# Four heads' quarters at once, or two: the order of score products and masks in a latent-attention layer

## The chip, the cores and the metric

The kernel runs on one core of a Trainium2 chip. The metric is the device time of one execution in microseconds. Three runs of the kernel before took 2292.64, 2293.26 and 2297.32 us, with a median of 2293.26 us. A core has a matrix engine (TensorE, "PE" in the profile; its weight loads are "PEld"), a vector engine (VectorE, "DVE"), a scalar engine (ScalarE, "ACT"), a general engine (GpSimd, "POOL") and a queue engine (SyncE, "SP") that here only issues DMAs. Each engine works through its own instructions in order; engines wait for each other through semaphores.

## The reference

Eight stages in a row work on x of shape (2, 1024, 128) in fp32. Each adds its result to x, and each begins with a layer norm of x: attention with one shared key and value head (layer "a"), a dense FFN with fp6-quantized operands, causal attention ("b"), the same dense FFN, causal attention whose keys and values come from a 32-wide latent ("c"), a mixture of 8 experts, causal attention with biases ("d"), and the mixture of experts again. All attentions have 16 heads of width 64 and 1024 positions. The layer that matters here is "c":

```python
latent_bll = jnp.einsum('bld,dc->blc', x_bld, Wkv_down)
k_blhd = jnp.einsum('blc,chk->blhk', latent_bll, Wk_up)
v_blhd = jnp.einsum('blc,chk->blhk', latent_bll, Wv_up)
attn = jnp.einsum('bqhd,bkhd->bhqk', q_blhd, k_blhd) / jnp.sqrt(jnp.asarray(HD, dtype=x_bld.dtype))
mask = (jnp.arange(l)[None, :] <= jnp.arange(l)[:, None])[None, None]
attn = jax.nn.softmax(jnp.where(mask, attn, neg_inf), axis=-1)
```

The scores of a head have the width 64 as their sum, but k is a product with the 32-wide latent, so the kernel folds Wk_up into the query projection once. A score is then a sum over 32 numbers, and one score product fills only a quarter of TensorE's 128 rows.

## The kernel before

**Units and steps.** An attention layer is worked in 16 units: two batches times eight pairs of heads. The units of layer c are c0 to c15 here; the profile's names (sc_c, pr_c, nmax_c) carry only the letter. A causal unit has five steps, each with one or two tiles of 128 queries, so that a step has about the same number of keys: the query tiles [7], [6, 0], [5, 1], [4, 2] and [3] (CAUSAL_STEPS). Layer c thus has 80 steps.

**One step.** The function `scores` issues, for the two heads h of the pair, the score products into two tiles `sc`, one of 128 x 1024 fp32 in PSUM for each head. There are two such buffers in all (pool ps_s), so head h of a step has to wait until ScalarE has read head h of the step before. Each head's products come in two halves, `lower` and `upper`, which write different PSUM banks. In layers a, b and d a half uses 64 of the 128 rows (ROWS), so two products run side by side; in layer c it uses a quarter (QUARTERS[2 * h + half], 32 rows), so that head 0 has quarters 0 and 1 and head 1 has quarters 2 and 3. `in_turn` deals out the products of several generators in turn, one of each. In fp32 each product appears in the profile as two matmuls (two passes).

The causal mask is added on TensorE: a product of an identity with a matrix of -2^100 above the diagonal is accumulated onto the scores of the diagonal tile. In layers b and d it uses a half of the rows and is part of the generators. In layer c (`mask`, L653) it uses all 128 rows in bf16, one matmul for each query tile of the step.

Behind each head's products, VectorE takes the negated maximum of each row (`nmax`, L682), ScalarE takes the exponential with that as bias and sums it (L697), VectorE inverts the sum (`rec`, L704, one for both heads, issued in the next step), and GpSimd scales the exponentials (L708). Two steps later the scaled tiles are transposed: blocks of 32 on VectorE into `slots` (L778), moved to their places by 16 DMAs on SyncE's queue (`blocks_moved`, L753), and the remaining tiles on TensorE (`pp`, L794), copied out by ScalarE. The product with the values (`av`, L845 in layer c) follows.

**What sets the order.** The order in each engine's queue is written out by hand in the loop over steps: transposes of the step two back with `normalize` of the last step inside them, the additions to x, `scores` and `exponentials` of the new step, the output products, a part of the next unit's projection, parts of the "side" work (norms, FFN or experts of the other batch), and up to four value products (`weigh_some(4)`). VectorE therefore runs transposes, rec and then the maxima of the new step, and TensorE runs pp, the scores, the output product or projection, side work, av.

**The lines of the change.** In `scores`, layer c (`latent`) issues the products of both heads, all four generators in turn, then the masks of head 0 and of head 1, before the loop over heads. In that loop the other layers issue their two generators for the head, and every layer issues the maxima.

Of the kernel before, what the change touches and what calls it, by code (L numbers as in the profile page):

```python
# [36 lines left out]
def kernel(ctx: ExitStack, tc: tile.TileContext, a: dict, out: bass.AP):  # L37
# [571 lines left out]
    def keys(u, qt):  # L609
        return qt + 1 if layers[u[0]]["causal"] else NT  # L610
# [12 lines left out]
    def scores(st):  # L623


        u, qts, at, k = st["u"], st["qts"], st["at"], st["k"]
        causal, latent = layers[u[0]]["causal"], layers[u[0]]["kind"] == "latent"
        sc = [ps_s.tile([P, 2 * QB], F32, tag="sc", name=f"sc_{k}_{h}") for h in range(2)]

        def operands(h, half):  # L630
            if latent:
                return QUARTERS[2 * h + half], qT[u][0], kT[u]
            x = 1 if h != half else 0
            return ROWS[half], qT[u][x], kT[u][x]

        def product(h, half, qt, k0, k1, diagonal):
            r, q, kk = operands(h, half)
            yield nc.tensor.matmul(  # L638
                sc[h][:, at[qt] + k0 : at[qt] + k1], lhsT=q[r, qt * P : (qt + 1) * P],
                rhs=kk[r, k0:k1], start=True, stop=not diagonal,  # L640
            )
            d = at[qt] + qt * P
            for f in range(P // DH if diagonal and not latent else 0):
                yield nc.tensor.matmul(  # L644
                    sc[h][:, d + f * DH : d + P], lhsT=unit[r, f, :], rhs=over[r, f, f * DH :],
                    start=False, stop=(f == P // DH - 1),
                )

        def mask(h):

            for qt in reversed(qts):
                d = at[qt] + qt * P
                nc.tensor.matmul(  # L653
                    sc[h][:, d : d + P], lhsT=ident_b, rhs=over_all, start=False, stop=True
                )

        def lower(h):

            yield from product(h, 0, qts[0], 0, QB - at[qts[0]], False)
            if len(qts) == 2:  # L660
                yield from product(h, 0, qts[1], 0, keys(u, qts[1]) * P, True)

        def upper(h):
            mid = QB - at[qts[0]]
            yield from product(h, 1, qts[0], mid, keys(u, qts[0]) * P, causal)

        def in_turn(gens):
            while gens:
                gens = [g for g in gens if next(g, None) is not None]

        if latent:
            in_turn([half(h) for h in range(2) for half in (lower, upper)])
            for h in range(2):
                mask(h)
        nmaxs = []
        for h in range(2):
            if not latent:
                in_turn([lower(h), upper(h)])
            nmax = small.tile([P, len(qts)], F32, tag="nmax", name=f"nmax_{k}_{h}")
            for n, qt in enumerate(qts):  # L680
                c = slice(at[qt], at[qt] + keys(u, qt) * P)
                nc.vector.tensor_reduce(  # L682
                    out=nmax[:, n : n + 1], in_=sc[h][:, c], axis=AX.X, op=ALU.max, negate=True
                )
            nmaxs.append(nmax)
        return sc, nmaxs
# [356 lines left out]
    lower = const.tile([P, NE, NE], F32, tag="lower", name="lower")  # L1043
# [46 lines left out]
    for step, (n, u, qts, i, total) in enumerate([*steps, *[(None, None, None, 0, 1)] * 4]):  # L1090
# [48 lines left out]
        if new:  # L1139
            sc, nmaxs = scores(new)  # L1140
            for h in range(2):
                exponentials(new, h, sc[h], nmaxs[h])
            last_step.append(new)
            waiting.append(new)
# [89 lines left out]
```

## Time and profile before

| | |
|---|---|
| median of three runs | 2293.26 us |
| profiled execution, its own time | 2291.09 us |
| its span, first to last instruction | 2289.4 us |
| mean clock granted to TensorE | 0.971 |
| layer c, from c0's first score product to the last step's end | 1178.4 to about 1656 us |
| units of layer c, first product to first product | 25.5 us (c6) to 36.4 us (c13) |

The profiled execution is 2.2 us below the median. Times inside the profile are counted from the first instruction. The page splits the span in 40 slices, about 57 us each; layer c is the slices 21 to 29. A row of the timeline merges neighbouring instructions of the same kind; its first column is the start, its second the length, and in square brackets stands how long the engine had been idle before and what ended that. In the waits, the three numbers are microseconds in all, times, and the longest. TensorE's clock falls to half for stretches of 3.4 or 6.8 us, most of them in layer c; a matmul then takes twice as long.

### The profile page before, as it was taken

What the parts mean: (1) busy time and instruction counts of PE and PEld (TensorE: products, weight loads), DVE (VectorE), ACT (ScalarE), POOL (GpSimd) and SP (SyncE); (2) the same over time, 40 slices, a digit from 0 to 9 for tenths busy, and PEclk for the clock granted to TensorE, in tenths of its full rate; (3) what the DMA queues carried; (4) which work ended last, traced back from release to release, by engine and by line L of the source; (5) the groups of instructions that cost most, each with busy time, mean ns of one, the idle gap of its engine ahead of it and who ended that gap; (6) DMA issues with size and microseconds to landing.
All of it is one profiled execution on the core that took longest, in us unless ns stands there. A gap on an engine that the chain in (4) does not pass through costs nothing.

```text
span 2289.4 us, 43111 instructions
## 1 busy us (share of the span) xinstructions
PE 2103.5 (92%) x14833; PEld 1231.8 (54%) x14833; DVE 1691.4 (74%) x2375; ACT 1492.9 (65%) x3340; POOL 1294.1 (57%) x1723
## 2 busy tenths in 40 slices
PE   6999999999998999999997888888889999999986
PEld 2454444444445666666654444444455666656663
DVE  7978999999886876678668877766766656766544
ACT  5777777667865666666655566655666557666652
POOL 4757777668765555465546655555644446544441
PEclk9999999999999999999998899999999999999998
DMA  5666666556676666666655556644665556646450
GB/s 140 145 150 155 159 154 149 131 131 150 153 189 152 149 160 162 161 155 154 147 131 124 129 130 139 141 109 103 171 157 133 122 119 158 161 118 145 111 139 10
DMA packets 144632, 320.42 MB, mean 140 GB/s; under 512 B 48288, under 2 KB 58784, under 8 KB 144416
## 3 DMA queue, kind: packets, MB, share of 16 engines
q1 hardware_dynamic: 144416, 317.67, 58.8%
q8 instruction: 120, 1.97, 0.4%
q14 instruction: 96, 0.79, 0.1%
HBM read 10.27 MB, written 2.10 MB: 5 GB/s over the span
## 4 chain that ended last, share of the span: by engine, by line
PE 58%; DVE 12%; SPq 9%; POOL 6%; ACT 5%; DMA 5%; issue 5%; DVEq 0%; ACTq 0%; POOLq 0%
SPq L753 9%; PE sc_a L638 7%; PE av_a L850 7%; PE av_d L850 5%; PE sc_b L638 5%; PE av_b L850 4%; PE sc_d L638 4%; DVE slots L778 4%; DMA prT<-slots 4%; ACT pr_c L697 2%; PE sc_c L638 2%; POOL pr_a L708 2%; DVE nmax_d L682 2%; DVE nmax_c L682 2%; PE pp_d L794 2%
## 5 line engine op out<-in xcount | busy, mean ns | idle before, releaser
L708 POOL TENSOR_SCALAR pr_a<-pr_a,rec_a 128x1024 f32<-128x1024 f32 x256 | 284.1, 1122 | 189.3 <-DVE rec_a L704 183.4
L697 ACT ACTIVATE pr_a<-sc_a,nmax_a 128x1024 f32<-128x1024 f32 x256 | 283.2, 1111 | 162.5 <-DVE nmax_a L682 94.1
L708 POOL TENSOR_SCALAR pr_d<-pr_d,rec_d 128x1024 f32<-128x1024 f32 (+7 forms) x256 | 187.0, 748 | 265.9 <-DVE rec_d L704 265.9
L682 DVE TENSOR_REDUCE nmax_a<-sc_a 128x1 f32<-128x1024 f32 x256 | 300.0, 1212 | 49.7 <-PE sc_a L638 49.6
L708 POOL TENSOR_SCALAR pr_b<-pr_b,rec_b 128x1024 f32<-128x1024 f32 (+7 forms) x256 | 190.0, 760 | 216.0 <-DVE rec_b L704 215.8
L682 DVE TENSOR_REDUCE nmax_d<-sc_d 128x1 f32<-128x1024 f32 (+7 forms) x256 | 177.4, 750 | 173.0 <-PE sc_d L644 172.3
L708 POOL TENSOR_SCALAR pr_c<-pr_c,rec_c 128x1024 f32<-128x1024 f32 (+7 forms) x256 | 188.4, 754 | 195.7 <-DVE rec_c L704 195.7
L697 ACT ACTIVATE pr_c<-sc_c,nmax_c 128x1024 f32<-128x1024 f32 (+7 forms) x256 | 186.5, 739 | 146.2 <-DVE nmax_c L682 118.1
L697 ACT ACTIVATE pr_b<-sc_b,nmax_b 128x1024 f32<-128x1024 f32 (+7 forms) x256 | 186.6, 739 | 142.8 <-DVE nmax_b L682 102.8
L697 ACT ACTIVATE pr_d<-sc_d,nmax_d 128x1024 f32<-128x1024 f32 (+7 forms) x256 | 186.6, 739 | 131.6 <-DVE nmax_d L682 117.6
L778 DVE STREAM_TRANSPOSE slots<-pr_a 128x1792 f32<-128x1792 f32 x128 | 261.0, 2039 | 12.7 <-POOL pr_a L708 8.7
L638 PE MATMUL sc_a<-k_a,q_a 64*128 64x512 f32 x512 | 261.3, 629 | 1.7 <-ACT pr_a L697 1.7
L682 DVE TENSOR_REDUCE nmax_b<-sc_b 128x1 f32<-128x1024 f32 (+7 forms) x256 | 177.1, 749 | 111.6 <-PE sc_b L644 110.6
L638 PE MATMUL sc_a<-k_a,qx_a 64*128 64x512 f32 x512 | 258.6, 629 | 0.0
L682 DVE TENSOR_REDUCE nmax_c<-sc_c 128x1 f32<-128x1024 f32 (+7 forms) x256 | 177.3, 750 | 97.7 <-PE sc_c L653 97.7
L850 PE MATMUL av_a<-prT,v_a 128*64 128x256 f32 x1792 | 223.2, 388 | 3.7 <-DMA prT<-slots 1.4
L850 PEld LDWEIGHTS av_a<-prT,v_a 128*64 128x64 f32 x1792 | 121.1, 137 | 122.7 <-issue 70.2
L638 PE MATMUL sc_d<-k_d,q_d 64*128 64x512 f32 (+3 forms) x416 | 158.9, 494 | 0.3 <-ACT pr_d L697 0.3
L638 PE MATMUL sc_b<-k_b,q_b 64*128 64x512 f32 (+3 forms) x416 | 158.8, 494 | 0.0
L638 PE MATMUL sc_b<-kx_b,qx_b 64*128 64x512 f32 (+3 forms) x416 | 153.3, 488 | 0.1
L638 PE MATMUL sc_d<-kx_d,qx_d 64*128 64x512 f32 (+3 forms) x416 | 153.2, 488 | 0.2
L778 DVE STREAM_TRANSPOSE slots<-pr_b 128x2048 f32<-128x2048 f32 (+1 forms) x64 | 121.8, 1903 | 12.0 <-DMA prT<-slots 8.8
(408 smaller groups left out, 4765.1 us busy)
## 6 DMA issues: line engine op xcount, KB each, us to landing
prT<-slots SPq DMA_DIRECT2D x768, 128.0 KB, 2.3
prT<-slots SPq DMA_DIRECT2D x832, 112.0 KB, 2.2
prT<-slots SPq DMA_DIRECT2D x768, 96.0 KB, 2.1
qx_b<-q_b SPq DMA_DIRECT2D x32, 256.0 KB, 3.6
kx_b<-k_b SPq DMA_DIRECT2D x32, 256.0 KB, 3.6
qx_d<-q_d SPq DMA_DIRECT2D x32, 256.0 KB, 3.7
kx_d<-k_d SPq DMA_DIRECT2D x32, 256.0 KB, 3.5
x<-in_x SPq DMA_DIRECT2D x4, 256.0 KB, 3.8
```

The costliest lines, as they stand in the source:

```text
L638: yield nc.tensor.matmul(sc[h][:, at[qt] + k0 : at[qt] + k1], lhsT=q[r, qt * P : (qt + 1) * P], rhs=kk[r, k0:k1], start=True, stop=not dia ...
L682: nc.vector.tensor_reduce(out=nmax[:, n : n + 1], in_=sc[h][:, c], axis=AX.X, op=ALU.max, negate=True)
L697: nc.scalar.activation(tiles_of(st, qt)[:, :, h, :], sc[:, c].rearrange("p (k q) -> p k q", q=P), AF.Exp, bias=nmax[:, n : n + 1], accum_o ...
L708: nc.gpsimd.tensor_scalar(out=pt, in0=pt, scalar1=rec[:, h, n : n + 1], scalar2=1.0, op0=ALU.mult, op1=ALU.mult,)
L753: nc.sync.dma_start(out=o, in_=x)
L778: nc.vector.transpose(dst, tiles[:, :n].rearrange("p k h (r q) -> p (k h) r q", q=32),)
L794: nc.tensor.transpose(pt[:, h, kt - k0, :], tiles[:, kt, h, :], ident)
L850: nc.tensor.matmul(shaped(av[ROWS[h], n], t0), lhsT=vs[u][:, kt, h, :], rhs=moving(h, kt, t0), start=(kt == 0), stop=(kt == nkt - 1),)
```

## The change

In layer c, each head now has its own turn: its lower and upper halves side by side (two quarters of TensorE's rows), its masks right behind, and its maxima. Only then do the products of head 1 follow. The number, the shapes and the operands of all instructions stay the same, and nothing outside `scores` is touched; in layers a, b and d nothing changes.

```diff
@@ -668,14 +668,11 @@
             while gens:
                 gens = [g for g in gens if next(g, None) is not None]
 
-        if latent:
-            in_turn([half(h) for h in range(2) for half in (lower, upper)])
-            for h in range(2):
-                mask(h)
         nmaxs = []
         for h in range(2):
-            if not latent:
-                in_turn([lower(h), upper(h)])
+            in_turn([lower(h), upper(h)])
+            if latent:
+                mask(h)
             nmax = small.tile([P, len(qts)], F32, tag="nmax", name=f"nmax_{k}_{h}")
             for n, qt in enumerate(qts):
                 c = slice(at[qt], at[qt] + keys(u, qt) * P)
```

On TensorE's queue the order of a step is before: the passes of both heads mixed, the masks of head 0, the masks of head 1. It is now: the passes of head 0, the masks of head 0, the passes of head 1, the masks of head 1. On the other engines the order is the same.

## The prediction

> **What bounds the kernel now.** I read the page first: engine shares, then the slices.
>
> ```profile
> span 2289.4 us, 43111 instructions
> ...
> PE 2103.5 (92%) x14833; PEld 1231.8 (54%) x14833; DVE 1691.4 (74%) x2375; ACT 1492.9 (65%) x3340; POOL 1294.1 (57%) x1723
> ```
>
> TensorE is busiest, but shares are averages, and the change touches only layer c. So next the busy times of layers b, c and d:
>
> ```profile
> core 0: us, PE busy (x) PEld busy (x) DVE busy (x) ACT busy (x) POOL busy (x), PEclk, DMA share, GB/s
> 641.00:1147.00 506.00, 489.92 (x3664) 320.66 (x3662) 365.52 (x538) 332.64 (x811) 277.24 (x400) 0.99 0.67 159
> 1178.00:1656.00 478.00, 402.08 (x3306) 224.90 (x3305) 356.09 (x549) 303.03 (x777) 272.84 (x411) 0.93 0.55 130
> 1660.00:2200.00 540.00, 517.29 (x3795) 336.82 (x3796) 341.27 (x533) 344.18 (x820) 265.04 (x392) 1.00 0.58 138
> ```
>
> TensorE fills b to 97% and d to 96%, but c only to 84%, at a granted clock of 0.93. It idles 76 us there; no engine is full. A chain of waits between engines sets c's time. The waits of that stretch:
>
> ```profile
> POOL pr_c L708 <- DVE rec_c L704: 195.7, 64, 7.0
> ACT pr_c L697 <- DVE nmax_c L682: 118.1, 62, 4.7
> DVE nmax_c L682 <- PE sc_c L653: 97.7, 66, 5.1
> PEld sc_c L638 <- ACT pr_c L697: 51.5, 65, 1.4
> PEld pp_c L794 <- POOL pr_c L708: 38.9, 38, 3.7
> ```
>
> The ring is visible: maxima wait for the masks, exponentials for maxima, the next scores for exponentials (they free the PSUM buffer), pp for GpSimd. The timeline of unit c7 shows the two kinds of step; TensorE first, then VectorE:
>
> ```profile
> 1382.95 1.14 PE L638 MATMUL sc_c<-latT,q_c 32*128 32x512 f32 x8
> 1384.03 0.28 PE L653 MATMUL sc_c<-over_all,ident_b 128*128 128x128 bf16 x2
> 1384.15 1.08 PE L533 MATMUL pq_c<-xT,wq_c 128*128 128x512 f32 x2
> ...
> 1393.21 1.13 PE L638 MATMUL sc_c<-latT,q_c 32*128 32x256 f32 x4 [0.93 <-ACT pr_c L697]
> 1394.55 1.13 PE L638 MATMUL sc_c<-latT,q_c 32*128 32x256 f32 x8 [0.21 <-ACT pr_c L697]
> 1395.61 0.40 PE L653 MATMUL sc_c<-over_all,ident_b 128*128 128x128 bf16 x4
> ```
>
> ```profile
> 1394.93 0.14 DVE L704 RECIPROCAL rec_c<-tot_c 128x4 f32<-128x4 f32 x1
> 1395.93 2.49 DVE L682 TENSOR_REDUCE nmax_c<-sc_c 128x1 f32<-128x768 f32 x4 [0.86 <-PE sc_c L653]
> ```
>
> In the first step ([7]) all four quarters stream together; the first mask is 1.08 us behind the first product. In the second ([5,1]) head 0's products run alone, 1.13 us, then TensorE waits until ScalarE frees head 1's buffer, and head 0's mask stands behind head 1's products: 2.40 us. VectorE has been ready 0.86 us by then.
>
> I sorted the 80 steps of the timeline by that distance. In 33 the quarters run together. In 5 steps [7] (c2, c3, c4, c9, c15) they do so at half clock (products 2.09 us long). In 42 the heads lie more or less apart.
>
> **The change part by part.** No instruction is added or removed; no DMA, GpSimd or ScalarE instruction is reordered, and nothing new is waited for. SyncE's and GpSimd's queues keep their order.
>
> *Head 0's mask moves ahead of head 1's products.* Head 0 alone needs 1.07 us to its mask (0.65 in step [3]): each quarter streams two passes of 512 columns, 0.53 us each, whether two or four quarters run. So in the 33 together-steps and the 5 at half clock VectorE gets head 0 no earlier. In the 42 apart-steps it gets it earlier by up to 1.3 us, of which only VectorE's idle time counts; the smaller of the two, step by step, sums to 25.6 us. In ten of them VectorE is busy until later and the gain is nothing.
>
> *Head 1's products move behind head 0's mask.* Layer b already works head by head: a whole step [7] there, from 840.60 to 842.77 us, takes TensorE 2.17 us for both heads, against 1.20 in c7. For c I take per head 1.07 plus 0.06 per mask: 2.27 or 2.40 for both heads. So TensorE is busy longer by 1.07 in a together-step (0.66 in [3]), 32.5 us over the 33; by 2 us in each half-clock step, 10 us; and by about 1.4 us over the 42, where head 1 waits for ScalarE in any case. In all 44 us. The new mask split has no row in layer c; bounds are 2.17 per step (layer b) and the 2.58 of an apart-step; mine lies between.
>
> Queued behind it on TensorE are the output product or projection, side work, av, pp, then the next scores. VectorE waits for head 1: it comes 1.2 us behind head 0, and the maxima of head 0 take 1.24 us. That fits with 0.04 us to spare.
>
> The Trainium skill, page "TensorEngine Tiling (Array Packing)", section "Key Properties", speaks against the change: switching the tiling mode drains TensorE, and masks on 128 rows between products on 32 rows switch twice as often. The trace puts a drain at about 0.1 us (in layer b a mask on its own rows starts 0.43 us behind the second pass of 512 columns, from 841.14 to 841.57; in c 0.53); an estimate from the rule with that row is 80 steps times 0.2, 16 us more of TensorE time.
>
> **How much reaches the end.** I carried both shifts through the timelines. A later TensorE costs nothing where it idles before the next scores, and an earlier VectorE gains nothing where the next scores are held by something else. Two units in full:
>
> c7. [7] ends 1.07 later; av waits 1.66 for a DMA behind it: absorbed. [6,0] 1.08 later; 0.93 idle (for the exponentials) absorbs all but 0.15. [5,1]: maxima 0.86 earlier. [4,2]: its scores had waited 0.55 for these exponentials; rec is 0.86 earlier, and head 0's mask no longer waits for head 1, so maxima start 1.8 earlier. The unit's end hangs on rec of [4,2]: GpSimd scales 2.7 us, pp waits (0.21 and 0.90 idle), next unit. c7 gains 1.8.
>
> c6. [7] costs 1.07, 0.47 idle follows: [6,0] starts 0.6 later, its first mask is now at 1.07 instead of 1.31, so its maxima are 0.4 later; [5,1] recovers that and gains 0.4; between [5,1] and [4,2] TensorE has no idle time and runs 0.36 late, which eats [4,2]'s gain. End: 0.
>
> By the same steps c5 gains 1.05, c8 0.85, c10 0.5, c12 0.7, c14 0.3. c0, c1, c2, c11 and c13 gain nothing: in c11 and c13 all the steps but one stand together, and the extra 1.07 fits into waits of 1.21 to 1.70 for VectorE's expert work; c1 and c2 end in GpSimd waits of 3.9 and 5.0 us. Sum: 5.2 us. In c3, c4, c9 and c15 step [7] runs at half clock: if it still does, 2 us more of TensorE time pass on and they lose 0.5, 1.1, 0.4 and 1.0; if the clock is full, they gain 0.5, 0.3, 0.5 and 0.8. So -2.2 or -7.3 us; the middle is -4.8. The slow steps follow GpSimd waits of 2 to 5 us at a unit's end, which mostly stay, while a fuller TensorE elsewhere speaks for fewer of them; hence the middle.
>
> The Trainium skill, "TensorE: Matmul & The Clock Gate", section "Part 1: The HAM clock gate (the "warmup" mystery)", says that the clock falls to half after an idle window of about 3.4 us. The trace has stretches of that length, but some behind windows that were 70% busy; by the rule alone the four slow starts stay, and the sum would be -2.2.
>
> The profiled execution took 2291.09 us, 2.2 below the median of the three. 2291.09 - 4.8 + 2.2 = 2288.5 us.
>
> **The rivals.**
>
> *TensorE passes its extra time on (slower).* Place: step [7] and what follows it in each unit. Behind [7] TensorE has no or little idle time in 11 units: what is left of the 1.07 (2.0 at half clock) is 0.5, 2, 2, 2, 1.07, 0.6, 0.53, 1.65, 1.07, 1.07 and 2.0 in c1 to c6, c8, c9, c12, c14, c15: 14.5 us. If no later step recovers it: 2307.8. It decides if the maxima of [5,1] don't come earlier by more than [7] makes them later, about 0.5 us. For it: no idle time behind many [5,1] steps. Against: the 0.86 us that VectorE idles before [5,1] in most units.
>
> *All cancels.* Gains stop at GpSimd's scaling and at DMAs, losses in idle time: 2293, within 0.2%. For it: c6, and the five units at 0. To be told from no change, this kernel's time must move by more than about 0.2%, 4.6 us.
>
> *TensorE gets as full as in layer b (much faster).* Busy 402 + 44 = 446 us at b's 97% is 460 instead of 478: 2275. For it: the same order runs in b. Against: c's units end on GpSimd and VectorE, whose waits layer c has more of.
>
> *The masks were not what VectorE waits for.* Then the 25.6 us don't exist and only TensorE's extra is left; it ends between the first two rivals. The wait row above, 97.7 us for L653, speaks against it.
>
> **How the numbers follow.** Small gain (2280 to 2290) 0.37; cancels 0.23; extra passed on, 2300 to 2315, 0.30; as full as b, 0.10. The first lies partly within 0.2%, the last two not. Faster by over 0.2%: 0.41; within 0.2%: 0.25; slower: 0.34. The likeliest is 2288.5, and its own range is 2281 to 2293. The full range takes in the slower rival with the longer drain of some us, and most of the faster one: 2271 to 2314.
>
> **What would show it.** Right: in c's waits, maxima waiting for L653 fall from 97.7 to 70 to 80 us; PE busy in c rises to 430 to 446; together-steps are gone and each step's products take 2.2 to 2.4 us; c5, c7 and c8 are about 1 us shorter; the layers around c keep their lengths. Wrong: maxima that wait for head 1's mask in the middle of a step (the 0.04 us of spare is gone); head 0's mask later than 1.1 us; [7] to [6,0] longer by the full 1.07 in most units and not made good; or the clock of c well away from 0.93, which moves more than the order does.

## The result: slightly slower, and the profile after

The changed kernel takes 2299.23 us (median), the kernel before, on the same chip, 2294.74 us. The ratio is 1.002, with a 95% interval of 1.0011 to 1.003: 4.5 us slower where 4.8 us faster was forecast. The profiled execution took 2298.51 us.

First the page of the changed kernel, its span and busy times:

```profile
span 2296.8 us, 43111 instructions
...
PE 2153.4 (94%) x14833; PEld 1255.2 (55%) x14833; DVE 1694.5 (74%) x2375; ACT 1496.3 (65%) x3340; POOL 1289.1 (56%) x1723
```

TensorE is busy 50 us longer, each of the other engines within 5 us of before. Then the same three stretches (layers b, c and d), by windows:

```profile
core 0: us, PE busy (x) PEld busy (x) DVE busy (x) ACT busy (x) POOL busy (x), PEclk, DMA share, GB/s
641.00:1147.00 506.00, 489.26 (x3670) 320.82 (x3666) 367.31 (x540) 333.35 (x811) 275.95 (x400) 1.00 0.67 160
1178.00:1656.00 478.00, 441.12 (x3206) 241.00 (x3202) 349.68 (x535) 295.46 (x747) 262.47 (x397) 0.91 0.53 125
1660.00:2200.00 540.00, 522.19 (x3815) 339.43 (x3813) 341.55 (x532) 346.51 (x826) 267.40 (x396) 0.99 0.59 140
```

Layer b is as it was. In c TensorE's busy time rises from 402 to 441 us and its clock falls from 0.93 to 0.91, but the layer is no longer over at 1656: it has fewer matmuls inside that window (3206, not 3306). From c0's first product to the last exponential it takes 491.8 us (1173.6 to 1665.4), where it took 477.3 us before.

These 14.4 us are more than the 7.4 us between the two profiled executions. Outside c the profiled execution before was 7.0 us longer (4.8 in front of c, 2.2 behind it), where the code is the same. The other kernels profiled below begin c at 1174 to 1177 us too, so the 1178.4 of the first profile was the odd one. The 14.4 us, of one profiled execution each, show where in c time goes, and the medians what it is worth.

The waits in layer c, in us in all, times, and the longest:

```profile
POOL pr_c L705 <- DVE rec_c L701: 206.2, 65, 8.2
ACT pr_c L694 <- DVE nmax_c L679: 120.3, 72, 4.7
DVE nmax_c L679 <- PE sc_c L653: 104.8, 57, 6.3
PEld L653 <- issue: 70.2, 126, 1.5
PEld pp_c L791 <- POOL pr_c L705: 33.6, 32, 3.3
...
PEld sc_c L638 <- ACT pr_c L694: 5.0, 16, 0.4
```

(Lines lie three lower than before: maxima are L679, exponentials L694.) TensorE's wait for the exponentials is gone: 51.5 us before, 5.0 now. But VectorE waits for the masks 104.8 us, not less than the 97.7 of before. They come early within a step, and the step itself comes late. Both are to be seen in unit c7, first on TensorE, then on VectorE:

```profile
1382.63 1.13 PE L638 MATMUL sc_c<-latT,q_c 32*128 32x512 f32 x4
1383.69 0.23 PE L653 MATMUL sc_c<-over_all,ident_b 128*128 128x128 bf16 x1
1383.85 1.13 PE L638 MATMUL sc_c<-latT,q_c 32*128 32x512 f32 x4
1384.91 0.23 PE L653 MATMUL sc_c<-over_all,ident_b 128*128 128x128 bf16 x1
1384.98 1.08 PE L533 MATMUL pq_c<-xT,wq_c 128*128 128x512 f32 x2
1388.24 1.74 PE L842 MATMUL av_c<-prT,lat_c 128*32 128x256 f32 x16 [2.19 <-DMA prT<-slots]
1389.91 1.97 PE L791 MATMUL pp_c<-ident,pr_c 128*128 128x128 f32 x8
1391.81 1.16 PE L638 MATMUL sc_c<-latT,q_c 32*128 32x384 f32 x6
...
1396.30 1.13 PE L638 MATMUL sc_c<-latT,q_c 32*128 32x256 f32 x6
1397.36 0.28 PE L653 MATMUL sc_c<-over_all,ident_b 128*128 128x128 bf16 x2
1397.57 1.13 PE L638 MATMUL sc_c<-latT,q_c 32*128 32x256 f32 x6
1398.63 0.28 PE L653 MATMUL sc_c<-over_all,ident_b 128*128 128x128 bf16 x2
```

```profile
1393.23 2.56 DVE L679 TENSOR_REDUCE nmax_c<-sc_c 128x1 f32<-128x896 f32 x4 [5.38 <-PE sc_c L653]
1395.71 2.30 DVE L775 STREAM_TRANSPOSE slots<-pr_c 128x2048 f32<-128x2048 f32 x1
1397.93 0.14 DVE L701 RECIPROCAL rec_c<-tot_c 128x4 f32<-128x4 f32 x1
1397.99 2.45 DVE L679 TENSOR_REDUCE nmax_c<-sc_c 128x1 f32<-128x768 f32 x4
```

Step [5,1] (from 1396.30) does what the change is for: head 0's mask stands 1.06 us behind the first product, head 1's products follow without a gap, and VectorE, which waited 0.86 us here before, goes straight from rec into the maxima. Step [7] (from 1382.63) has its mask at 1.06 as well, but the same product rows now last twice as long, 2.28 us to the second mask. Behind it TensorE waits 2.19 us for a DMA, is busy for only 1.21 us between 1384.90 and 1388.30, and falls to half clock: av takes 1.74 us and pp 1.97, where the same matmuls took 1.07 and 1.09 at full clock in c3 of before. Step [6,0] begins 9.18 us after [7] instead of 5.96, and VectorE waits 5.38 us for it.

Summed over the 16 units, from the start of each step to the start of the next ("score time" runs from a step's first product to the end of its last mask; "half clock" is the time at which the clock was 0.5, over the whole layer 71.7 us before and 85.3 after):

| stretch from step | before, us | after, us | what else changed |
|---|---|---|---|
| [7] | 90.8 | 118.8 | score time 27.3 to 50.5; half clock 15.8 to 46.7 |
| [6,0] | 78.7 | 78.3 | TensorE's idle time 13.6 to 0.4 |
| [5,1] | 122.0 | 111.0 | half clock 32.1 to 11.7 |
| [4,2] | 100.6 | 107.3 | score time 33.0 to 44.2 |
| [3], 15 of them | 80.7 | 73.3 | TensorE's idle time 29.6 to 17.9 |

So there are gains, 11.0 us behind [5,1] (some of it from a better clock there) and 7.4 behind [3], and step [7] alone loses 28.0. Seven of its 16 stretches, those with half clock in c2, c3, c4, c7, c8, c10 and c15, carry 21.8 of these; the other nine have 6.1 together, 0.7 each. Five of the seven (c2, c3, c4, c10 and c15, 16.5 us together) are at half clock when [7] begins, as five were before (c9 in place of c10). In c7 and c8 the clock falls only behind [7].

### The profile page after: what moved, and what is told of

Read it like the earlier page. It is cut to its first block, busy times and chain, and to the rows that moved or that the text cites. A ratio compares the mean times of both kernels' runs of the same rounds, so it can differ in the third digit from the quotient of the medians.

```text
span 2296.8 us, 43111 instructions
## 1 busy us (share of the span) xinstructions
PE 2153.4 (94%) x14833; PEld 1255.2 (55%) x14833; DVE 1694.5 (74%) x2375; ACT 1496.3 (65%) x3340; POOL 1289.1 (56%) x1723
## 3 DMA queue, kind: packets, MB, share of 16 engines
q8 instruction: 120, 1.97, 0.4%
## 4 chain that ended last, share of the span: by engine, by line
PE 57%; DVE 13%; SPq 11%; POOL 5%; DMA 5%; issue 4%; ACT 4%; DVEq 0%; ACTq 0%; POOLq 0%
SPq L750 11%; PE sc_a L638 7%; PE av_a L847 7%; DVE slots L775 5%; PE av_d L847 5%; PE sc_d L638 4%; PE av_b L847 4%; PE sc_b L638 4%; DMA prT<-slots 4%; PE sc_c L638 3%; POOL pr_c L705 2%; DVE nmax_d L679 2%; PE av_c L842 2%; PE pp_d L791 2%; POOL pr_a L705 1%
## 5 line engine op out<-in xcount | busy, mean ns | idle before, releaser
L694 ACT ACTIVATE pr_a<-sc_a,nmax_a 128x1024 f32<-128x1024 f32 x256 | 283.1, 1110 | 163.9 <-DVE nmax_a L679 94.4
L679 DVE TENSOR_REDUCE nmax_a<-sc_a 128x1 f32<-128x1024 f32 x256 | 300.0, 1212 | 51.0 <-PE sc_a L638 50.8
L679 DVE TENSOR_REDUCE nmax_d<-sc_d 128x1 f32<-128x1024 f32 (+7 forms) x256 | 177.5, 750 | 170.6 <-PE sc_d L644 169.9
L694 ACT ACTIVATE pr_b<-sc_b,nmax_b 128x1024 f32<-128x1024 f32 (+7 forms) x256 | 186.6, 739 | 142.7 <-DVE nmax_b L679 107.5
L694 ACT ACTIVATE pr_c<-sc_c,nmax_c 128x1024 f32<-128x1024 f32 (+7 forms) x256 | 187.0, 740 | 141.4 <-DVE nmax_c L679 121.6
L694 ACT ACTIVATE pr_d<-sc_d,nmax_d 128x1024 f32<-128x1024 f32 (+7 forms) x256 | 186.6, 739 | 132.0 <-DVE nmax_d L679 118.9
L679 DVE TENSOR_REDUCE nmax_c<-sc_c 128x1 f32<-128x1024 f32 (+7 forms) x256 | 182.5, 751 | 106.7 <-PE sc_c L653 105.2
L679 DVE TENSOR_REDUCE nmax_b<-sc_b 128x1 f32<-128x1024 f32 (+7 forms) x256 | 177.1, 748 | 108.5 <-PE sc_b L644 107.5
```

The source lines that it names most:

```text
L679: nc.vector.tensor_reduce(out=nmax[:, n : n + 1], in_=sc[h][:, c], axis=AX.X, op=ALU.max, negate=True)
L694: nc.scalar.activation(tiles_of(st, qt)[:, :, h, :], sc[:, c].rearrange("p (k q) -> p k q", q=P), AF.Exp, bias=nmax[:, n : n + 1], accum_o ...
```

## Does the clock follow the order? Two theories of the loss

Unit c3 stands at half clock in both kernels when [7] begins. TensorE's timeline of the changed kernel:

```profile
1267.47 2.08 PE L638 MATMUL sc_c<-latT,q_c 32*128 32x512 f32 x4
1269.48 0.29 PE L653 MATMUL sc_c<-over_all,ident_b 128*128 128x128 bf16 x1
1269.70 2.08 PE L638 MATMUL sc_c<-latT,q_c 32*128 32x512 f32 x4
1271.71 0.29 PE L653 MATMUL sc_c<-over_all,ident_b 128*128 128x128 bf16 x1
1271.79 2.02 PE L533 MATMUL pq_c<-xT,wq_c 128*128 128x512 f32 x2
1273.74 1.94 PE L842 MATMUL av_c<-prT,lat_c 128*32 128x256 f32 x16
```

and of the kernel before:

```profile
1271.38 2.09 PE L638 MATMUL sc_c<-latT,q_c 32*128 32x512 f32 x8
1273.40 0.39 PE L653 MATMUL sc_c<-over_all,ident_b 128*128 128x128 bf16 x2
1273.59 1.30 PE L533 MATMUL pq_c<-xT,wq_c 128*128 128x512 f32 x2
1274.82 1.07 PE L845 MATMUL av_c<-prT,lat_c 128*32 128x256 f32 x16
```

Before, the clock is back 2.5 us into the step. After, the projection and av still run at half, and it is back after 8.2 us. The windows, cut where the clock changes (the clock stands behind the busy times of the five engines), after:

```profile
1265.50:1268.90 3.40, 2.47 (x8) 1.22 (x8) 3.33 (x4) 0.86 (x2) 2.54 (x2) 0.50 0.09 19
1268.90:1272.30 3.40, 3.40 (x9) 1.14 (x8) 2.55 (x4) 1.03 (x2) 2.05 (x3) 0.50 0.24 57
1272.30:1275.70 3.40, 3.40 (x19) 0.69 (x18) 2.36 (x4) 1.87 (x5) 0.90 (x1) 0.50 0.62 148
1275.70:1279.10 3.40, 3.40 (x23) 2.35 (x24) 0.99 (x1) 1.07 (x2) 1.31 (x2) 0.98 0.66 159
```

and before:

```profile
1267.10:1270.50 3.40, 0.85 (x3) 0.46 (x4) 3.33 (x5) 1.71 (x5) 3.40 (x5) 0.51 0.68 157
1270.50:1273.90 3.40, 3.40 (x15) 1.56 (x16) 3.37 (x5) 0.86 (x2) 1.44 (x1) 0.50 0.02 5
1273.90:1277.30 3.40, 3.40 (x29) 1.71 (x29) 3.37 (x6) 2.13 (x4) 2.06 (x3) 0.98 0.45 106
```

Before, one window in which TensorE is busy throughout (3.40 of 3.40) is followed by full clock. After, TensorE is busy throughout from 1268.90 to 1272.30, and the next window still has 0.50. What differs is what ran: four quarters at a time before, and after, for 2.73 us of that window, two quarters, half of the rows.

c3 is not alone. In layer c of the changed kernel six windows at half clock have TensorE busy throughout and half clock again behind them: in [7] of c2, c3, c4, c10 and c15 and in [4,2] of c12. Each holds 2.1 to 3.1 us of two-quarter products. In the kernel before there is no such window: [7] of c2, c3, c4 and c15 and [4,2] of c12, at half clock too, are back at full clock behind their first window that is busy throughout, and [7] of c9 behind one with 3.17 us busy. So the stretches at half clock last 3.4 or 6.8 us in layer c before, and up to 13.7 us after. What makes the clock fall is less clear: in both kernels it falls behind windows in which TensorE was partly idle, behind [7] of c7 with 1.21 and behind [7] of c8 with 2.65 of 3.40 us busy.

**Theory 1**: the clock goes by the rows at work, so products on half of the rows bring it back later or let it fall. Its narrower form (1a) says that this holds at equal TensorE time. **Theory 2**: the clock is a bystander; what costs is TensorE's extra time in [7], or the wait for DMAs behind it, in units with no slack.

## Experiment 1: step [7] with all four quarters again

```diff
-        if latent:
+        together = latent and qts[0] == 7
+        if together:
             in_turn([half(h) for h in range(2) for half in (lower, upper)])
...
-            if not latent:
+            if not together:
                 in_turn([lower(h), upper(h)])
+                if latent:
+                    mask(h)
```

(against the kernel before; the condition in the first line is all that changes in experiments 2 and 6 to 9.)

> Step [7] of every layer-c unit keeps the order of before (all four quarters, then the masks); the other four steps have the new order. Theory 1: the loss of the change sits at step [7], where the two-quarter products hold TensorE twice as long and the half clock lasts longer behind it; the other steps gain. Then the intervals from [7] to [6,0] go back from 118.8 to about 91 us in sum, half-clock time behind [7] from 47 to about 16 us, the gains behind [5,1] (11 us) and [3] (7 us) stay, and layer c is 8 to 15 us shorter than before: ratio 0.994 to 0.997. Theory 2: every step's extra TensorE time is passed on alike, [7] is one of five: then about a third of the loss goes, ratio 1.000 to 1.002.

Measured: 2289.46 us, ratio 0.9979 (0.9966 to 0.9992). With [7] undone, the change gains, though less than Theory 1 expected. Between the two ratios lie 0.41%, 9.4 us. The stretch behind [7] is 100.1 us (before 90.8, the change 118.8), its half clock 24.3 us (15.8 and 46.7); the stretch behind [4,2] is longer than in the change, 112.4 us. TensorE waits longer for the DMAs there, 9.3 us in sum, which keeps Theory 2 alive.

## Experiment 2: only step [7] apart

The condition is `qts[0] != 7`.

> The other half: only step [7] has the new order, the other four steps keep all four quarters together. Theory 1 (the loss sits at [7] with the clock): 18 to 28 us more, ratio 1.007 to 1.012, slower than the whole change. Theory 2 (every step's extra counts alike): 16 steps of 1.1 us, partly absorbed, 5 to 10 us, ratio 1.002 to 1.004.

Measured: 2327.14 us, ratio 1.0145 (1.0127 to 1.0162). It is more than expected, 32.5 us. The window of the whole layer c (its clock is 0.85):

```profile
1176.10:1691.90 515.80, 452.72 (x3304) 238.83 (x3302) 357.09 (x549) 304.50 (x774) 271.93 (x411) 0.85 0.51 120
```

Half clock lasts 153.6 us, 78.7 of them behind [7], whose stretches sum to 129.8 us. So [7] apart is the harmful part, and with the other steps apart as well its harm is smaller (the change: 4.5 us). The parts do not add: 32.5 alone and a gain of 5 for the rest would be 27 us. Why the half clock spreads so far here wasn't taken apart.

## Experiments 3 and 4: equal TensorE time, half or all of the rows

Both keep the order of before, but let only two products run at a time. In experiment 3 each head has one quarter:

```diff
-                return QUARTERS[2 * h + half], qT[u][0], kT[u]
+                return QUARTERS[2 * h], qT[u][0], kT[u]
```

> The order of before, but each head puts both halves on one quarter, so two products run at a time on 64 of the 128 rows and the masks stay behind both heads. This is the TensorE price of the change without its earlier mask. Theory 1a (the clock goes by how many rows work, not by how long TensorE is busy): half-clock time in layer c of 85 us or more, well above that of the twin run on two halves. Theory 1b (the clock goes by TensorE's idle time alone): half-clock time like the twin's within 10 us. Both: slower than before, ratio 1.008 to 1.025, since the first mask comes at 2.1 us in every step.

In experiment 4 each head has a half, with its 32 rows of latent and query twice below each other, and half the scale to make up for it:

```diff
-                nc.scalar.mul(q[:, cols], pp, SCALE)
+                nc.scalar.mul(q[:, cols], pp, SCALE / 2 if latent else SCALE)
...
-                return QUARTERS[2 * h + half], qT[u][0], kT[u]
+                return ROWS[h], qT[u][0], kT[u]
```

> As the two-quarter run, but each product runs over 64 rows (both copies of the head's query and latent, with the query's scale halved), so two products at a time use all 128 rows; the same passes, order and widths otherwise. Theory 1a (rows count for the clock): half-clock time in layer c clearly below the two-quarter run's, by 20 us or more, and the time 8 us or more shorter than that run's. Theory 1b (idle time alone counts): the same time as the two-quarter run within 3 us and the same half-clock time within 10 us.

Measured: 2354.81 us, ratio 1.026 (1.0239 to 1.0281), with the quarters, and 2334.23 us, ratio 1.0171 (1.0151 to 1.019), with the halves. Layer c by windows, the quarters first:

```profile
1174.50:1720.60 546.10, 495.88 (x3303) 277.76 (x3302) 356.28 (x549) 301.53 (x773) 272.13 (x411) 0.88 0.49 114
```

```profile
1175.10:1700.70 525.60, 466.05 (x3303) 263.42 (x3302) 356.50 (x549) 300.60 (x774) 272.24 (x411) 0.96 0.50 118
```

The two have as many passes, and a [7] at full clock mostly has its masks at 1.94 and 2.00 us in both. Nor are the products on halves the faster ones: [6,0], at full clock in both, has a score time of 41.6 us with the quarters and 44.5 us with the halves. What differs is the rows at work, 64 or 128 of 128 (and with them the rows of one product, 32 or 64): the clock is 0.88 or 0.96, the half clock 129.7 or 37.5 us, and the time 20.6 us apart. That is what 1a forecast; the run with the quarters is a little slower than expected.

With the quarters the clock even falls out of a window that is busy throughout, nearly all of it score products of a step whose heads lie apart, so that mostly one quarter works at a time (from 1669.01 to 1672.33 us):

```profile
1669.05:1672.45 3.40, 3.40 (x16) 1.86 (x17) 2.40 (x3) 1.99 (x6) 2.27 (x9) 1.00 0.49 116
1672.50:1675.90 3.40, 3.40 (x35) 2.28 (x32) 3.32 (x5) 1.91 (x5) 3.04 (x9) 0.50 0.00 0
```

The Trainium skill, page "TensorE: Matmul & The Clock Gate", section "Part 1: The HAM clock gate (the "warmup" mystery)", says that the ratio is set by how busy TensorE has lately been, in windows of about 3.4 us. The length of the windows agrees with the 3.40 us seen here; "busy" doesn't suffice: in the change's c3, 3.40 us of 3.40 busy, 2.73 of them on half of the rows, left the clock at 0.50.

## Experiment 5: the order of the change, on all rows

Against the changed kernel: each half of a head takes 64 rows, head 1 with a copy of the query whose two halves are exchanged, which costs two DMAs for each unit.

```diff
-        qx = None if latent else qkp.tile([P, S], F32, tag="qx", name=f"qx_{k}")
+        qx = qkp.tile([P, S], F32, tag="qx", name=f"qx_{k}")
...
-                nc.scalar.mul(q[:, cols], pp, SCALE)
+                nc.scalar.mul(q[:, cols], pp, SCALE / 2 if latent else SCALE)
...
-            elif hf == NQB - 1 and not latent:
+            elif hf == NQB - 1:
...
-                return QUARTERS[2 * h + half], qT[u][0], kT[u]
+                return ROWS[half], qT[u][1 if h != half else 0], kT[u]
```

> The whole new order, but each score product runs over 64 rows instead of 32: head h's halves use the two halves of the rows, with an exchanged copy of the queries for the other half (two more DMAs of 256 KB in each unit on SyncE's queue) and half the query scale. The same passes and masks in the same order, all 128 rows at work. Theory 1 (the change loses through the half clock that two-quarter products keep): half-clock time in layer c from 85 us to 45 or less, layer c 12 to 25 us shorter than with the change, ratio to the kernel before 0.992 to 0.998. Theory 2 (it loses through the longer score products themselves): those stay, so ratio 1.001 to 1.004, the half clock notwithstanding.

Measured: 2284.66 us, ratio 0.9964 (0.995 to 0.9978). Layer c by windows, and VectorE's wait for the masks:

```profile
1175.50:1649.80 474.30, 434.39 (x3298) 241.72 (x3298) 359.83 (x549) 304.90 (x774) 271.24 (x411) 0.96 0.62 147
```

```profile
DVE nmax_c L679 <- PE sc_c L653: 87.6, 53, 5.1
```

The order and the number of passes of the change are kept, and the layer becomes 17.4 us shorter than in the change, with half clock down from 85.3 to 34.1 us and a clock of 0.96. Between the ratios lie 0.56%, some 13 us. [6,0] is at full clock in both, and its score time is 42.0 us in both, so the products on 64 rows are not faster in themselves. So the rows at work make the difference between a loss and a gain, and Theory 2 doesn't suffice.

It has its share, though. Behind [7] the half clock is 15.0 us here, as before the change (15.8), and the score time 46.8 us, nearly that of the change (50.5). The stretches there sum to 104.8 us: 14.0 more than before for TensorE's extra time, and the change's 118.8 are another 14.0 for the clock. Here later steps make the first 14.0 good; in the change they don't make good both. A second reading: experiment 4 has the same rows and two products at a time in the old order, and takes 2334.23 us. Head by head with the mask behind it is worth 47 to 50 us where only two products run at a time anyway. What the old order had for it was that four quarters ran at once.

## Experiments 6 to 9: which steps gain

The condition is now `qts[0] not in (5, 3)`: [5,1] and [3] apart, the others as before.

> Only steps [5,1] and [3], where the second head mostly waits for ScalarE anyway, have the new order; [7], [6,0] and [4,2] keep four quarters together. Theory 1 (the mask's wait is worth removing where the heads lie apart, and all other steps only lose TensorE time and clock): the gains behind [5,1] and [3] of about 10 us each stay, the 12 us lost behind [4,2] in the run with only [7] together go; half-clock time in layer c 60 us or less; ratio 0.993 to 0.997, faster than that run. Rival (the gains are given back at the DMA wait behind [7]): ratio 0.998 to 1.000, and TensorE's DMA wait behind [7] rises to 10 us or more.

Then `qts[0] in (7, 6)`: [5,1], [4,2] and [3] apart.

> Steps [5,1], [4,2] and [3] have the new order, [7] and [6,0] keep four quarters together. Against the run with only [7] together it tells what [6,0] is worth, against the run with [5,1] and [3] what [4,2] is worth. Theory 1: [6,0] costs TensorE 14 us in new order and gains nothing, but has 14 us of idle time behind it, so it is worth 0 to 4 us; ratio 0.996 to 0.998, between the other two.

Then [5,1] alone (`qts[0] != 5`) and [3] alone (`qts[0] != 3`).

> Only step [5,1] has the new order. If the gain of the run with [5,1] and [3] (0.9948) lies at [5,1], where the heads lie apart in 13 of the 16 units of the kernel before, this run keeps most of it: 0.994 to 0.997. If it lies at the unit's end, behind [3]: 0.998 to 1.000.

> Only step [3] has the new order. If the gain lies at [5,1]: 0.998 to 1.001, since the unit's end hangs on GpSimd's scaling of step [4,2] and not on [3]. If it lies at the unit's end: 0.994 to 0.997.

| steps apart | time, us | ratio to before | 95% interval |
|---|---|---|---|
| [5,1] and [3] | 2281.65 | 0.9948 | 0.9934 to 0.9961 |
| [5,1] | 2282.44 | 0.9962 | 0.9949 to 0.9975 |
| [5,1], [4,2] and [3] | 2286.2 | 0.9972 | 0.9961 to 0.9984 |
| all but [7] (experiment 1) | 2289.46 | 0.9979 | 0.9966 to 0.9992 |
| [3] | 2294.34 | 1.0009 | 0.9997 to 1.0021 |
| all (the change) | 2299.23 | 1.002 | 1.0011 to 1.003 |
| [7] | 2327.14 | 1.0145 | 1.0127 to 1.0162 |

(The medians of the kernel before beside them lie between 2291.34 and 2294.74 us, so the ratios are what compares.) The gain is that of [5,1]; [3] alone gives nothing that can be measured. [4,2] apart costs a little, 0.24% between the first row and the third: its stretches are 108.9 us where it is apart ([5,1], [4,2] and [3]) and 99.7 where it isn't ([5,1] and [3]), its score time rising from 31.7 to 44.6 us with 4.8 us of idle time to take it. Most of that returns behind [3], whose stretches are 72.6 us then and 82.1 otherwise (82.4 with [3] alone apart, 80.7 before). So the 7.4 us that the change gained behind [3] come with [4,2] apart, not with [3], and the 10 us expected behind [3] in the first run of these did not come. [6,0] is worth 0.07% between the third row and the fourth, within the noise. The first three rows lie too close for an order among neighbours, but the version with [5,1] and [3] has the lowest ratio here and beats both kernels. Layer c and two of its waits (the maxima are L685 here, the exponentials L700):

```profile
1174.80:1646.20 471.40, 409.15 (x3299) 231.29 (x3298) 355.49 (x549) 302.17 (x774) 270.67 (x410) 0.92 0.56 131
```

```profile
DVE nmax_c L685 <- PE sc_c L653: 87.8, 53, 5.1
...
PEld sc_c L638 <- ACT pr_c L700: 32.5, 59, 1.6
```

TensorE is busy 409 us (454 in the change, from the first product to the last exponential), half clock is 75.1 us (71.7 before; 60 or less was expected), and the waits for masks are 10 us shorter than before. So the gain of [5,1] is one of order: it needs no less half clock in all. With [5,1] alone the half clock is 71.7 us, exactly that of before.

## Experiment 10: the values a step later

Behind [7] TensorE may wait for the DMAs that move transposed blocks (9.3 us in experiment 1). If that wait feeds the half clock, values taken a step later should mend it. To the kernel of experiment 1:

```diff
-                    x["ready"] = step + (2 if blocked(st["u"], qb) else 0)
+                    x["ready"] = step + ((3 if st["u"][0] == 2 else 2) if blocked(st["u"], qb) else 0)
```

> As the run with only [7] together, but layer c's value products of a block moved by DMA are released three steps after its last transpose instead of two, so that TensorE doesn't meet the DMAs behind [7]. DMA theory (the 16 issues of 0.63 us on SyncE's queue hold the unit's joint, and the gains of the later steps end in that wait): TensorE's wait for prT behind [7] falls from 9.3 to under 2 us, the half-clock time behind it from 24 to under 16, and the time falls by 4 to 10 us below that run's, ratio 0.993 to 0.996. Rival (the wait is hidden): the same time within 2 us, the idle time moves elsewhere.

Measured: 2328.1 us, ratio 1.0148 (1.0128 to 1.0168). The DMA wait behind [7] did fall, from 9.3 to 1.2 us, and the half clock there from 24.3 to 15.0. But a new wait took its place, for ScalarE to copy out the single PSUM buffer of av:

```profile
PEld av_c L848 <- ACT attnT_c L864: 44.1, 15, 6.2
PE av_c L848 <- ACT attnT_c L864: 37.0, 15, 5.8
```

(The two lines are the weight loads and the matmuls of one wait, not a sum.) The run is inconclusive on the price of the DMA wait. In the change, though, that wait is 4.5 us behind [7] in sum, and 4.6 before: by its own length it isn't what the change lost. Whether it made the clock fall in c7, where it stands in the window in front of the fall, is open.

## Why the prediction was wrong, point by point

**The mechanism on VectorE was right.** Head 0's mask comes 1.06 us behind the first product in every step at full clock (1.07 said; 0.63 in [3], 0.65 said). The last mask is at 2.28 us in [7] and 2.40 in [6,0], [5,1] and [4,2] (2.27 and 2.40 said). Head 1 just fits: VectorE waits 0.00 us for its mask in the median (0.04 us of spare said), 0.10 in [3]. TensorE's busy time in the window of c is 441 us (430 to 446 said), but that window ends before the layer does: from the first product to the last exponential it is 454.2 us after 401.5, so 53 us more and not 44. With all rows at work (experiment 5) it is 434.5 us. And VectorE's idle time leaves nothing to gain in seven of the 42 apart-steps, where the prediction counted ten; its sum of 25.6 us stands.

**Unit by unit it was near where [7] and [4,2] run at full clock.** The eight units with neither slow in the change (c0, c1, c5, c6, c9, c11, c13, c14) change by -1.23 us in sum; the prediction's terms for them give -1.85. c5 gained 1.70 (1.05 said), but its [4,2] also lost 3.41 us of half clock. c9, whose [7] is at full clock now, lost 0.76 (a gain of 0.5 said for that case). c0, c1, c11, c13 moved by -0.16 to 0.46 (0 said): their slack took the extra 1.07. The other eight became 15.7 us longer. The sum was -2.2 or -7.3, -4.8 in the middle; it came to +14.4 by the stretches of two executions that differ by 7.0 us the other way outside c, and to +4.5 by the medians.

**The step that failed** is "the slow steps follow GpSimd waits of 2 to 5 us at a unit's end, which mostly stay, while a fuller TensorE elsewhere speaks for fewer of them; hence the middle". TensorE became fuller and the half clock longer: five [7]s still began slow, with c10 in place of c9. A slow [7] was priced at "2 us more of TensorE time"; in the changed kernel the stretches from a slow [7] lengthened by 3.1 us on average (21.8 over seven), because, in the five that began slow, the products on half of the rows don't bring the clock back and what stands behind them runs slow too. And in c7 and c8 the clock fell behind a [7] that began at full clock, which no term allowed for; their 5.3 us are in the 21.8, and why it fell there is open. In the change the half clock behind [7] tripled, and this cost 14.0 us, by experiment 5 (one profiled execution each).

**The size without that step** can be read, with care, from experiment 5: -0.36% with an interval of -0.50 to -0.22%, that is -11.5 to -5.0 us, against the -7.3 that the prediction gave for a full clock in [7]. The care is that this kernel has less half clock than before in the other steps (19.1 us for 55.9), so some of its gain is not the order's.

**A second, smaller miss**: the maxima's wait for masks was to fall from 97.7 to 70 to 80 us and rose to 104.8. Part is the clock: on all rows it is 87.6. By steps, VectorE's idle time before a step's first maxima fell in [5,1] from 11.2 to 1.8 us and in [4,2] from 30.3 to 23.2, but rose in [6,0], which a late [7] pushes back, from 23.5 to 41.8 (5.38 us of it in c7; 31.6 in sum on all rows). [4,2] was taken for a gainer in c7; over all units its stretch lost 6.6 us, and [3] behind it won back 7.4.

**The rivals.** "TensorE passes its extra time on" named the right place, [7] and what follows it. Its sum there, 14.5 us, is close to what experiment 5 measured for TensorE's time alone (14.0), and it is recovered later, as the forecast had it against the rival; the clock's 14.0 on top are not. The result lies between "all cancels" (2293) and this rival (2307.8). "As full as layer b" fell: TensorE is fuller, but at half clock. "The masks were not what VectorE waits for" fell with experiments 6 and 8, where the early mask in [5,1] gains 0.52 and 0.38%. The sign that it named last, a clock "which moves more than the order does", is the one that came.

## What to carry to other kernels

Taking row groups apart is paid twice: in the time of the passes, and in a clock that here went by the rows at work. So put such an edit only into steps whose groups lie apart already (here [5,1], whose second head waits for a buffer), or first fill the rows, with the operands doubled and half the scale. A price for a slow step must include what stands behind it, until rows enough have run for the clock to return.

## What the runs showed of the hardware

- **TensorE's clock isn't granted by busy time alone.** With 64 of 128 rows at work the half clock lasted 129.7 us in layer c, with 128 rows 37.5 us, at equal pass counts. Windows at half clock, busy throughout, that were followed by half clock again: six in layer c of the change, none in experiment 5, which has its order on all rows. The only one in experiment 4, from 1584.40 to 1587.80 us, has a step whose heads lie apart, with 64-row products that run mostly one after another, on half of the rows. Where between 64 and 128 rows the bound lies was not measured, nor whether it is the rows as such or the work done in them.
- **A mask on all rows between products on quarters is cheap.** The next head's products start 0.16 us behind the mask (1383.69 to 1383.85 in c7), where a second mask of the same head starts 0.06 to 0.07 us behind the first: 0.1 us that we put down to the switch. The Trainium skill, page "TensorEngine Tiling (Array Packing)", section "Key Properties", says that a switch of the tiling mode drains TensorE; the rows agree with a drain of the size that the prediction estimated.
- **The half clock can spread from one edit.** Step [7] alone apart raised it from 71.7 to 153.6 us, more than all steps apart did (85.3). What spreads it there is open.
